# Softmax steps and key split of the second attention block re-ordered, and ScalarE's copy of the weighted values put ahead of a normalization in all later blocks

## The chip, the cores and the metric

The kernel runs on one core of a Trainium2 chip. The metric is device time in microseconds (us) of one execution. In the core, TensorE (PE) multiplies matrices into PSUM banks, VectorE (DVE) and ScalarE (ACT) take results out of PSUM and do elementwise work, GpSimd (POOL) does elementwise work on SBUF, and SyncE (SP) issues most DMA transfers. Each engine runs its instructions in the order of its queue.

## The reference

Four layers follow one another on 1024 tokens of 256 features (4 sequences of 256), each added to its input and normalized. The change touches only the first, attention with 16 heads:

```python
q = hidden_states @ Wq.T
k = hidden_states @ Wk.T
v = hidden_states @ Wv.T
# per head: 128 plain and 64 rotary features of q and k, 128 of v
q_rope = _apply_rope(q_rope, cos, sin)
k_rope = _apply_rope(k_rope, cos, sin)
scores = einsum('bqhd,bkhd->bhqk', q_nope, k_nope) / sqrt(DN) \
       + einsum('bqhd,bkhd->bhqk', q_rope, k_rope) / sqrt(DR)
attn = softmax(scores, axis=-1)
out = einsum('bhqk,bkhd->bqhd', attn, v)
return out.reshape(B, S, H * DV) @ Wo.T
```

After it come a gated feed-forward layer with a Walsh-Hadamard transform, an mLSTM block with its own feed-forward part, and a feed-forward layer with int8 weights. All results are float32.

## The kernel before

**Blocks.** Attention is cut into 16 blocks. Block h works on a pair of heads (h // 2) and one half of the tokens (h % 2: two sequences, 512 tokens). The main loop runs h = 0 to 14 and calls `first_block` for h = 0 and `fast_block` for the others; "the second block" is h = 1. A block computes the scores and softmax of its own pair and half, the projections of block h + 1, and the weighted values and output product of block h - 1, all interleaved. So the softmax of block h feeds the products V of block h + 1.

**Projections.** From h = 1 on they are the steps W0, W1 (values), R0, R1 (rotary parts of queries and keys), Q0, Q1 (plain queries of the two heads) and K0, K1 (plain keys). Each is two sums in two PSUM banks, built from inputs (`xp`) and weights (`wp`) that were split into a top part, a low part and a combination of them (`heads_of` L142, `rests_of` L156 to L158: three VectorE operations and a ScalarE cast per weight, then the DMA of the next pair's raw weight on SP). ScalarE copies the first bank (L521), VectorE joins the second to it (L523, L524). The bank is then free for the next step with the same tag. For rotary parts VectorE shuffles (L538), and GpSimd does three operations (L541 to L543).

**Softmax.** `scores` fills four banks, two with tag sc (first sequence, heads 0 and 1) and two with tag pt (second sequence): four quarters, numbered 0 to 3. `maxima` (VectorE, L610) takes the row maxima, `exponentials` (ScalarE, L619) the exponentials and their sums. `finish(k)` normalizes quarter k (reciprocal L627 on VectorE, multiplication on VectorE for even k, L632, on ScalarE for odd k, L630) and transposes it in blocks of 32 (VectorE, L640). `spread` then moves all four with 16 DMAs from SP into `prT`.

**Values and output.** `V00` to `V11` multiply prT with the values of the block before (first digit: sequence, second: head; L72 into `ps_ot`). After the second head ScalarE copies the sum to `oT` (`settled["across"]`, L687). `O0` and `O1` multiply oT with the output weight (L72 into `ps_mm`); each stands twice in the order, for its two halves of rows.

**What sets the order.** PE's order is written out by hand: `in_turn` ties each product behind the one before. In the second block it is `SECOND`, in the others `ORDER`:

```python
SECOND = "R0 W0 R1 W1 Q0 Q1 V00 V01 K0 V10 V11 K1 O0 O0 O1 O1".split()
ORDER = "W0 V00 V01 V10 V11 O0 O0 R0 R1 O1 O1 Q0 Q1 K0 K1 W1".split()
```

On the other engines a scheduler sets the order when the kernel is built, by the order of the code and its own estimate of when operands are ready, and `behind(ins)` puts what is traced under it behind `ins`, where both are on the same engine; it adds no wait of its own between engines. A block under `behind` that spans several engines is thus bound only on the engine of `ins`.

Of the kernel before, what the change touches and what calls it, by code (L numbers as in the profile page):

```python
# [23 lines left out]
NPAIR = H0 // 2  # L24
# [17 lines left out]
def tile_two_layers(ctx: ExitStack, tc: tile.TileContext, a: dict, out: bass.AP):  # L42
# [6 lines left out]
    def bank(tag):  # L49
        return psum.tile([P, 512], F32, tag=tag, name=f"ps_{tag}")  # L50
# [28 lines left out]
    def slot(k, shape, name, dtype=F32):  # L79
        return wts.tile(shape, dtype, tag=f"ff{k}", name=name)  # L80
# [6 lines left out]
    ps = bank("pt")  # L87
# [50 lines left out]
    def heads_of(p, name):  # L138

        top = attn.tile([P, KC, S], F32, tag="top", name="top")  # L140
        x, t = (raws[p, name], top) if name != "R" else (halves_first(raws[p, name]), pairs_first(top))
        return top, nc.vector.tensor_single_scalar(t.bitcast(I32), x.bitcast(I32), TOP, ALU.bitwise_and)  # L142
# [38 lines left out]
    def load_output(p):  # L181
        wo = attn.tile([P, 2, D], F32, tag="wo", name="w_o")
        nc.sync.dma_start(wo, a["w_o"][p])
        return wo
# [35 lines left out]
    settled = {}  # L220
    behind = lambda ins: tc.issue_after(ins.ins)
# [386 lines left out]
    def maxima(ps):  # L608
        nmax = small.tile([P, 2], F32, tag="nmax", name="nmax", bufs=5)
        nc.vector.tensor_reduce(  # L610
            nmax, ps.rearrange("p (t k) -> p t k", t=2), AX.X, ALU.max, negate=True
        )
        return nmax

    def exponentials(ps, nmax):
        pr = attn.tile([P, 2, S], F32, tag="pr", name="pr", bufs=5)
        rsum = small.tile([P, 2], F32, tag="rsum", name="rsum", bufs=5)
        for qt in range(2):
            nc.scalar.activation(  # L619
                pr[:, qt, :], ps[:, qt * S : (qt + 1) * S], AF.Exp,  # L620
                bias=nmax[:, qt : qt + 1], accum_out=rsum[:, qt : qt + 1],
            )
        return pr, rsum
# [18 lines left out]
    def spread(cross):  # L642

        prT = attn.tile([P, 2, 2, QB, 2, 2, 32], F32, tag="prT", name="prT")
        for c in range(QB):
            for r in range(QB):
                nc.sync.dma_start(
                    prT[32 * r : 32 * r + 32, :, :, c],
                    cross[32 * c : 32 * c + 32, :, r : XB : QB],
                )  # L650
        return {
            bb: [lambda kt, bb=bb, e=e: prT[:, bb, kt, :, e].rearrange("p c t q -> p t c q") for e in range(2)]
            for bb in range(2)
        }

    def crossing():
        return attn.tile([P, 2, XB, 2, 2, 32], F32, tag="cross", name="cross")
# [16 lines left out]
    def weighted(t, bb, e, probs, po):  # L674
        in_turn(
            lambda: mm_k(
                po[:, e * S : (e + 1) * S],
                lambda i: t[4][:, 2 * bb + i, e * P : (e + 1) * P],
                probs,
                2,  # L680
            )
        )

    def output_product(h, bb, po):

        oT = attn.tile([P, 2, S], F32, tag="oT", name="oT")
        settled["across"] = nc.scalar.copy(oT, po.rearrange("p (e s) -> p e s", e=2))  # L687
        p, n = divmod(h, 2)

        def halves():  # L690
            ps = bank("mm")
            for t in range(2):
                in_turn(
                    lambda: mm_k(
                        ps[:, t * D : (t + 1) * D],
                        lambda i: oT[:, i, t * P : (t + 1) * P],
                        lambda i: w_os[p][:, i, :],
                        2,
                    )
                )  # L700
                if not t:
                    yield
            rows = acc[n][:, 2 * bb : 2 * bb + 2, :]
            yield nc.vector.tensor_tensor(rows, ps.rearrange("p (t d) -> p t d", t=2), rows, ALU.add)

        steps = halves()
        return lambda: next(steps, None)
# [5 lines left out]
    def finisher(found, crossed):  # L713
        def finish(k):
            bb, e = divmod(k, 2)
            return block_transposed(normalized(*found[k], e), e, crossed[:, bb])
        return finish
# [31 lines left out]
    def fast_block(h, t, probs, prev, steps):  # L749

        po, outs, last = {}, {}, {}

        def take_step(name):
            last[name] = steps[name]()
            settled["block"] = last[name][1]
            return last[name]

        def value_step(bb, e):
            if not e:
                po[bb] = bank("ot")  # L760
            weighted(prev, bb, e, probs[bb][e], po[bb])
            if e:
                outs[bb] = output_product(h - 1, bb, po[bb])

        p = (h + 1) // 2
        ps = scores(t, (0, 1), (lambda: take_step("R0")) if h == 1 else nothing)
        crossed = crossing()
        top = [maxima(ps[bb][e]) for bb in range(2) for e in range(2)]
        found = [exponentials(ps[0][0], top[0])]
        finish = finisher(found, crossed)  # L770
        finish(0)
        for step in SECOND if h == 1 else ORDER:
            if step[0] == "V":
                value_step(int(step[1]), int(step[2]))
            elif step[0] == "O":
                settled["out"] = outs[int(step[1])]()
            elif step not in last:
                take_step(step)
            if step == "W0":
                copied, done = last["W0"]  # L780
                with behind(copied):
                    found.append(exponentials(ps[0][1], top[1]))
                    if h == 1:
                        found.append(exponentials(ps[1][0], top[2]))
                        found.append(exponentials(ps[1][1], top[3]))
                with behind(done):
                    finish(1)
            elif step == "R1" and h == 1:
                with behind(last["R1"][1]):
                    finish(2)  # L790
            elif step == "W1" and h == 1:
                with behind(last["W1"][1]):
                    settled["softmax"] = finish(3)
                out = spread(crossed)
            elif step == "V01" and h > 1:
                with behind(settled["across"]):
                    found.append(exponentials(ps[1][0], top[2]))
                finish(2)
            elif step == "V11" and h > 1:
                with behind(settled["across"]):  # L800
                    found.append(exponentials(ps[1][1], top[3]))
                settled["softmax"] = finish(3)
                if h > 1 and h % 2 and p < NPAIR:
                    with behind(settled["softmax"]):
                        split(p, "K")
                out = spread(crossed)
        return out

    def split(p, *names):
        tops = []  # L810
        for name in names:
            tops.append(heads_of(p, name))
        for name, (top, _) in zip(names, tops):
            last = rests_of(p, name, top)
        return last
# [25 lines left out]
    for h in range(NB - 1):  # L841
        if h:
            probs = fast_block(h, tiles, probs, prev, steps)
        else:
            probs = first_block(tiles, steps)
        with behind(settled["block"]):
            if h == 0:
                split(1, "Q", "K")
            elif h == 1:
                input_parts_of(1)  # L850
            elif h % 2 == 0 and h // 2 + 1 < NPAIR:
                split(h // 2 + 1, "R", "Q")
            if h % 2 and h // 2 + 2 < NPAIR:
                split(h // 2 + 2, "W")
        if h == 1:
            w2 = ff_weight("w2", 4)
            w2b = slot(3, [P, NH, D], "w2b")
        if h % 2 == 0:
            if 0 < h < NB - 2:
                w_os[h // 2 + 1] = load_output(h // 2 + 1)  # L860
        if h in (7, 9, 11):
            src, dst = (w2, w2b) if h == 7 else (dst, src)
            butterflies(1 << (h - 7) // 2, src, dst)
        prev, tiles = tiles, after_it
        if h + 2 < NB:
            after_it, steps = fast_projections(h + 2)
# [25 lines left out]
    ps, prs, outs = {}, {}, []  # L892
    for bb in range(2):
        ps.update(scores(tiles, (bb,)))
        top = [maxima(ps[bb][e]) for e in range(2)]
# [723 lines left out]
    split = tc.alloc_tile_pool(name="split", bufs=2, side="right")  # L1619
# [121 lines left out]
```

## Time and profile before

| what | value |
|---|---|
| median of three runs | 688.52 us |
| runs | 686.74, 688.93, 688.52 us |
| profiled execution | 689.46 us |
| its span, first to last instruction | 687.7 us |
| mean granted TensorE clock | 0.992 |
| busy share PE, DVE, ACT, POOL | 98%, 73%, 46%, 27% |
| score products of h = 1, 2, 3 start at | 37.88, 65.98, 89.81 us |

In the profile's rows a line number is that of the instruction in the kernel, or of a helper that many callers share (L72 is such a line). A timeline row gives start, duration, engine, line, operation, what is written and read, the count of merged instructions, and in brackets the idle time before it with what ended that. A row of the chain gives start, length and what filled that part of the chain. In a row of time slices the engines stand in the order PE, weight loads, DVE, ACT, POOL, then the granted TensorE clock, the DMA share and GB/s. A busy PE may still be slow or wait inside a merged row, so lengths of equal groups are compared.

### The profile page before, as it was taken

The numbers are of one execution on the slowest core, as the hardware profiler recorded it, in microseconds if no ns is written. First come the engines' busy times: TensorE is split into PE (matmuls) and PEld (weight loads), VectorE is DVE, ScalarE is ACT, GpSimd is POOL, SyncE is SP. The second block draws the span as 40 slices with busy tenths as digits, with TensorE's granted clock in tenths as the row PEclk, the third lists the DMA queues.
The fourth block names the chain that finished last, engine by engine and source line by source line (L and its number), as shares of the span: only waits on it lengthen the run. The fifth ranks groups of instructions, "written<-read, shape, count | busy, mean of one in ns | idle before, by whom it ended". The sixth has DMA issues, their size and how long they took to land.

```text
span 687.7 us, 9902 instructions
## 1 busy us (share of the span) xinstructions
PE 671.4 (98%) x3364; PEld 530.5 (77%) x3364; DVE 503.3 (73%) x1226; ACT 318.9 (46%) x823; POOL 187.4 (27%) x167
## 2 busy tenths in 40 slices
PE   9989999999999999999999999999999999999995
PEld 5878888888888888888888778745684568788785
DVE  6997777687787778777766796465679557966767
ACT  4545554554465455445535455156312651261652
POOL 4262224404426444364144410005000220000310
PEclk9999999999999999999999999999999999999998
DMA  7242334223332421431232540003121300001001
GB/s 247 90 93 52 111 85 92 49 68 84 66 85 51 108 62 40 99 78 31 47 62 51 195 101 34 1 0 124 40 84 62 123 1 1 0 1 62 0 1 62
DMA packets 56643, 45.44 MB, mean 66 GB/s; under 512 B 9968, under 2 KB 52112, under 8 KB 55440
## 3 DMA queue, kind: packets, MB, share of 16 engines
q1 hardware_dynamic: 55728, 41.00, 23.4%
q0 software_dynamic: 432, 3.15, 1.3%
q10 hardware_dynamic: 432, 0.66, 0.3%
q8 instruction: 27, 0.44, 0.3%
q14 instruction: 24, 0.20, 0.1%
HBM read 25.61 MB, written 1.08 MB: 39 GB/s over the span
## 4 chain that ended last, share of the span: by engine, by line
PE 81%; DVE 12%; ACT 4%; issue 1%; DMA 1%; POOL 0%; DVEq 0%; ACTq 0%
PE ps_mm L72 10%; PE ps_sc L515 8%; PE ps_d L72 7%; PE ps_ot L72 7%; PE ps_pt L515 5%; PE ps_d L1128 4%; PE ps_sc L587 4%; PE ps_pt L587 4%; PE ps_m L1069 4%; PE ps_d L1477 3%; PE ps_d L1069 3%; PE ps_mm L515 3%; PE ps_ot L556 3%; PE ps_mm L556 3%; PE ps_sc L599 2%; PE ps_m L72 2%
## 5 line engine op out<-in xcount | busy, mean ns | idle before, releaser
L541 POOL TENSOR_TENSOR rope_raw<-rope_raw,cst 128x512 f32<-128x512 f32 x28 | 38.4, 1370 | 203.8 <-DVE rope_swp L538 203.8
L515 PE MATMUL ps_sc<-xp,wp 128*128 128x512 f32 x246 | 69.3, 417 | 0.0
L72 PE MATMUL ps_mm<-w_o,oT 128*128 128x256 f32 x256 | 61.3, 384 | 1.7 <-ACT oT L687 1.4
L72 PEld LDWEIGHTS ps_mm<-w_o,oT 128*128 128x128 f32 x256 | 47.5, 189 | 13.2 <-ACT oT L687 6.9
L640 DVE STREAM_TRANSPOSE cross<-pr 128x512 f32<-128x512 f32 x60 | 42.3, 708 | 19.5 <-ACT pr L630 18.9
L72 PE MATMUL ps_ot<-prT,v 128*128 128x256 f32 x240 | 54.8, 380 | 0.5 <-issue 0.5
L515 PEld LDWEIGHTS ps_sc<-xp,wp 128*128 128x128 f32 x246 | 47.0, 192 | 9.5
L619 ACT ACTIVATE pr<-ps_sc,nmax 128x256 f32<-128x256 f32 x64 | 29.7, 472 | 50.0 <-DVE nmax L610 50.0
L1351 POOL TENSOR_TENSOR ex<-cst,ex 128x512 f32<-128x512 f32 x16 | 19.7, 1265 | 112.0 <-DMA ex<-far 112.0
L72 PEld LDWEIGHTS ps_ot<-prT,v 128*128 128x128 f32 x240 | 44.5, 190 | 6.8 <-issue 1.2
L515 PE MATMUL ps_pt<-xp,wp 128*128 128x512 f32 x162 | 41.5, 391 | 0.0
L542 POOL TENSOR_TENSOR rope_swp<-rope_swp,cst 128x512 f32<-128x512 f32 x28 | 36.4, 1299 | 0.0
L630 ACT ACTIVATE pr<-pr,rinv 128x256 f32<-128x256 f32 x60 | 27.2, 501 | 19.0 <-DVE rinv L627 18.9
L515 PEld LDWEIGHTS ps_pt<-xp,wp 128*128 128x128 f32 x162 | 30.4, 188 | 6.5
L610 DVE TENSOR_REDUCE nmax<-ps_sc 128x2 f32<-128x512 f32 x32 | 20.6, 686 | 15.6 <-PE ps_sc L599 15.5
L619 ACT ACTIVATE pr<-ps_pt,nmax 128x256 f32<-128x256 f32 x64 | 30.1, 485 | 2.8 <-DVE nmax L610 2.8
L587 PE MATMUL ps_sc<-kn,qn 128*128 128x256 f32 x128 | 30.3, 379 | 0.0
L587 PE MATMUL ps_pt<-kn,qn 128*128 128x256 f32 x128 | 30.2, 379 | 0.0
L72 PE MATMUL ps_d<-fm,w 128*128 128x512 f32 x64 | 29.4, 599 | 0.0
L1027 ACT ACTIVATE glu_g<-ps_d 128x512 f32<-128x512 f32 x16 | 9.5, 593 | 42.1 <-PE ps_d L72 42.1
L156 ACT CAST wp<-top 128x512 fp32r<-128x512 f32 x28 | 16.6, 618 | 26.7 <-DVE top L142 26.7
L1128 PE MATMUL ps_d<-w,hT 128*128 128x256 f32 x128 | 28.4, 379 | 0.0
(350 smaller groups left out, 1586.6 us busy)
## 6 DMA issues: line engine op xcount, KB each, us to landing
prT<-cross SPq DMA_DIRECT2D x240, 64.0 KB, 2.1
ex<-far SPq DMA_DIRECT2D x8, 512.0 KB, 5.4
w<-in_w SPq DMA_DIRECT2D x3, 1024.0 KB
w_o<-in_w_o SPq DMA_DIRECT2D x8, 256.0 KB, 5.1
rawR<-in_w_qkv SPq DMA_DIRECT2D x14, 128.0 KB, 2.6
rawW<-in_w_qkv SPq DMA_DIRECT2D x7, 256.0 KB, 3.0
rawQ<-in_w_qkv SPq DMA_DIRECT2D x7, 256.0 KB, 3.2
rawK<-in_w_qkv SPq DMA_DIRECT2D x7, 256.0 KB, 4.1
```

The lines of the kernel that those rows point to most:

```text
L72: last = nc.tensor.matmul(ps, lhsT=lhs(i), rhs=rhs(i), start=(i == 0), stop=(i == n - 1))
L515: lambda: nc.tensor.matmul(ps[at], lhsT=left(k, i), rhs=right(k, i), start=(m == 0), stop=(m == len(terms) - 1))
L541: nc.gpsimd.tensor_tensor(by_b(raw), by_b(raw), cs, ALU.mult)
L542: nc.gpsimd.tensor_tensor(by_b(swp), by_b(swp), sn, ALU.mult)
L556: lambda: nc.tensor.matmul(ps[at][:, t * S : (t + 1) * S], lhsT=xp[k][:, i, j * P : (j + 1) * P], rhs=part[:, k, i, :], start=(m == 0), st ...
L587: lambda: nc.tensor.matmul(ps[bb][e][:, qt * S : (qt + 1) * S], lhsT=qn[:, e, queries(bb, qt)], rhs=kn[:, e, keys(bb)], start=(qt == 0), s ...
L619: nc.scalar.activation(pr[:, qt, :], ps[:, qt * S : (qt + 1) * S], AF.Exp, bias=nmax[:, qt : qt + 1], accum_out=rsum[:, qt : qt + 1],)
L630: nc.scalar.mul(pr[:, qt, :], pr[:, qt, :], rinv[:, qt : qt + 1])
L640: return nc.vector.transpose(cross[:, :, e], pr.rearrange("p t (x i) -> p x t i", i=32))
L1069: nc.tensor.matmul(banks[name][:, batch(x)], lhsT=left, rhs=right, start=start and not x, stop=True, skip_group_check=True,)
L1128: lambda: nc.tensor.matmul(po, lhsT=hT[:, i, j * P : (j + 1) * P], rhs=wd[:, i, :], start=(i == 0), stop=(i == NH - 1),)
L1477: nc.tensor.matmul(ps, lhsT=lhs, rhs=rhs, start=(k == 0), stop=(k == len(terms) - 1))
```

## The change

In the second block the first quarter's normalization is no longer emitted right after its exponentials but behind W0's join. Exponentials 1, 2 and 3 go behind the copies of W0, R1 and W1 (before: all behind W0's). The finishes of quarters 0 to 3 go behind the joins of W0, R1, Q0 and Q1 (before: free, W0, R1, W1), and `spread` is emitted after Q1 and not after W1. The split of the second pair's key weights moves from the end of the first block (behind its last VectorE addition) into the second block, behind W1's join.

In the blocks from h = 2 the finish of quarter 1 is emitted at V01 and not at W0, and its ScalarE part is put behind the copy of the weighted values into oT; its VectorE part stays behind W0's join.

```diff
         found = [exponentials(ps[0][0], top[0])]
         finish = finisher(found, crossed)
-        finish(0)
+
+        def exponentials_behind(k, ins):
+            with behind(ins):
+                found.append(exponentials(ps[k // 2][k % 2], top[k]))
+
+        def finish_behind(k, ins):
+            with behind(ins):
+                settled["softmax"] = finish(k)
+
+        if h > 1:
+            finish(0)
         for step in SECOND if h == 1 else ORDER:
...
-            if step == "W0":
-                copied, done = last["W0"]
-                with behind(copied):
-                    found.append(exponentials(ps[0][1], top[1]))
-                    if h == 1:
-                        found.append(exponentials(ps[1][0], top[2]))
-                        found.append(exponentials(ps[1][1], top[3]))
-                with behind(done):
-                    finish(1)
-            elif step == "R1" and h == 1:
-                with behind(last["R1"][1]):
-                    finish(2)
-            elif step == "W1" and h == 1:
-                with behind(last["W1"][1]):
-                    settled["softmax"] = finish(3)
-                out = spread(crossed)
-            elif step == "V01" and h > 1:
+            if h == 1:
+                if step in ("W0", "R1", "W1"):
+                    copied, done = last[step]
+                    k = ("W0", "R1", "W1").index(step)
+                    exponentials_behind(k + 1, copied)
+                    if step == "W1":
+                        with behind(done):
+                            split(1, "K")
+                    else:
+                        finish_behind(k, done)
+                elif step in ("Q0", "Q1"):
+                    finish_behind(2 + int(step[1]), last[step][1])
+                    if step == "Q1":
+                        out = spread(crossed)
+            elif step == "W0":
+                exponentials_behind(1, last["W0"][0])
+            elif step == "V01":
                 with behind(settled["across"]):
-                    found.append(exponentials(ps[1][0], top[2]))
+                    finish_behind(1, last["W0"][1])
+                    exponentials_behind(2, settled["across"])
                 finish(2)
-            elif step == "V11" and h > 1:
-                with behind(settled["across"]):
-                    found.append(exponentials(ps[1][1], top[3]))
+            elif step == "V11":
+                exponentials_behind(3, settled["across"])
                 settled["softmax"] = finish(3)
...
             if h == 0:
-                split(1, "Q", "K")
+                split(1, "Q")
```

More of the change, by code (lines that the diff above doesn't have):

```diff
@@ L778, in fast_block @@
                 take_step(step)
-            if step == "W0":
-                copied, done = last["W0"]
-                with behind(copied):
-                    found.append(exponentials(ps[0][1], top[1]))
-                    if h == 1:
-                        found.append(exponentials(ps[1][0], top[2]))
-                        found.append(exponentials(ps[1][1], top[3]))
-                with behind(done):
-                    finish(1)
-            elif step == "R1" and h == 1:
-                with behind(last["R1"][1]):
-                    finish(2)
-            elif step == "W1" and h == 1:
-                with behind(last["W1"][1]):
-                    settled["softmax"] = finish(3)
-                out = spread(crossed)
-            elif step == "V01" and h > 1:
+            if h == 1:
[15 more added lines that the diff above has]
+            elif step == "V01":
                 with behind(settled["across"]):
-                    found.append(exponentials(ps[1][0], top[2]))
+                    finish_behind(1, last["W0"][1])
+                    exponentials_behind(2, settled["across"])
                 finish(2)
-            elif step == "V11" and h > 1:
-                with behind(settled["across"]):
-                    found.append(exponentials(ps[1][1], top[3]))
+            elif step == "V11":
+                exponentials_behind(3, settled["across"])
                 settled["softmax"] = finish(3)
-                if h > 1 and h % 2 and p < NPAIR:
+                if h % 2 and p < NPAIR:
                     with behind(settled["softmax"]):
```

## The prediction

> **What bounds the kernel now.** The page first: engine shares, then the chain that ended last.
>
> ```profile
> PE 671.4 (98%) x3364; PEld 530.5 (77%) x3364; DVE 503.3 (73%) x1226; ACT 318.9 (46%) x823; POOL 187.4 (27%) x167
> ...
> PE 81%; DVE 12%; ACT 4%; issue 1%; DMA 1%; POOL 0%; DVEq 0%; ACTq 0%
> ```
>
> PE is the bound, and the end moves only where PE stands still. So I followed the chain in order of time (start, length, what) through the second block (h = 1, scores from 37.9, next block's scores at 65.98) and an ordinary one (from 89.81):
>
> ```profile
> 38.84 2.74 DVE top L142 x2
> 41.58 2.31 DVE wp L157 x2
> ...
> 46.47 2.37 DVE nmax L610 x4
> ...
> 50.58 0.61 DVE v L523
> ...
> 51.23 0.97 PE ps_mm L556 x4
> 52.21 2.56 PE ps_sc L515 x6
> ...
> 100.30 1.99 PE ps_mm L72 x8
> ...
> 105.04 1.73 PE ps_mm L72 x8
> ```
>
> In the second block the chain leaves PE for DVE: splits of Q and K, row maxima, normalization, then the values' join (L523) that frees the bank W1 waits for. The six Q0 matmuls after it take 2.56 against 1.36 to 1.39 elsewhere. The last two lines are O0 and O1: same work, O0 0.26 longer. The waits of PE (us in total, times, longest):
>
> ```profile
> PE ps_mm L72 <- ACT oT L687: 1.4, 3, 0.5
> PE ps_mm L556 <- DVE v L523: 1.4, 1, 1.4
> PE ps_mm L556 <- ACT v L521: 0.8, 1, 0.8
> ```
>
> And the slices around the second block's stall (the figure after POOL is the granted clock):
>
> ```profile
> 50.00:51.00 1.00, 0.00 (x0) 0.00 (x0) 1.00 (x2) 1.00 (x5) 0.43 (x1) 1.00 0.00 0
> ...
> 52.00:53.00 1.00, 1.00 (x4) 0.81 (x4) 0.18 (x1) 1.00 (x3) 0.00 (x0) 0.50 0.00 0
> ```
>
> The stall cost twice: 0.8 + 1.4 of standing, then the clock: 0.78, 0.50, 0.50, 0.52 in the four us from 51, that is 0.22 + 0.50 + 0.50 + 0.48 = 1.7. Together 3.9.
>
> **Ordinary blocks (13, h = 2 to 14).** Why O0 is late, in the timeline:
>
> ```profile
> 98.72 0.12 DVE L627 RECIPROCAL rinv<-rsum 128x2 f32<-128x2 f32 x1
> 98.87 0.91 ACT L630 ACTIVATE pr<-pr,rinv 128x256 f32<-128x256 f32 x2 [0.98 <-DVE rinv L627]
> 99.69 0.56 ACT L687 COPY oT<-ps_ot 128x512 f32<-128x512 f32 x1
> ...
> 100.30 1.59 PEld L72 LDWEIGHTS ps_mm<-w_o,oT 128*128 128x128 f32 x8 [0.43 <-ACT oT L687]
> ```
>
> ScalarE stands 0.98 for the reciprocal, normalizes, and only then copies oT, though its product (V00, V01) left PE at 96.82 + 1.73 = 98.55. O0 reads that copy at 100.30. With the copy first it runs about 98.7 to 99.25, some 0.7 before V11 ends at 100.28: O0 follows without a gap, as O1 does. Gain: 13 x 0.26 = 3.4, plus the 1.4 of the three blocks where PE stood openly (h = 8, 10, 12): 4.8.
>
> What the moved wait holds up: ScalarE now stands at the copy until V01 ends; behind it are the normalization, two exponentials, the second copy. The copy leaves about 0.4 later than the reciprocal allows the normalization today, so the normalization ends near 100.0 instead of 99.73 and VectorE's transpose (99.81) starts 0.3 later; behind that transpose stands the reciprocal of the third quarter, which waits for an exponential until 101.21 anyhow. That exponential starts when copy and normalization are both done, now as before. Cover: 0.7 here; without it each us of lateness would be one at the prT transfers, which have (104.53 + 16 x 0.65 + 2.1 = 117.0, read by V00 at 120.66) 3.6 to spare. So nothing is charged. No DMA moves in these blocks.
>
> **The second block.** Removed from before the maxima: K's split. Its share of the two chain rows is half of 2.74 + 2.31, plus 0.6 of L158, about 3.1 at most; but Q's operations inherit some of the waiting on POOL that K's had. These lines show it:
>
> ```profile
> 20.81 0.41 DVE L142 TENSOR_SCALAR top<-rawR 128x512 int32<-128x512 int32 x1
> ...
> 40.08 1.50 DVE L142 TENSOR_SCALAR top<-rawK 128x512 int32<-128x512 int32 x1
> ...
> 57.53 1.29 DVE L640 STREAM_TRANSPOSE cross<-pr 128x512 f32<-128x512 f32 x2
> ```
>
> The same split step takes 0.41 alone and 1.50 while POOL turns the rotary keys; the two transposes took 0.64 each beside POOL too. So Q's L158 will wait as K's L142 did, maxima start at 44.6 instead of 46.37 (1.8 earlier), the values' copy at 46.2, W1's first bank is free before R1 ends at 47.8; the first normalization moves behind the values' join, which so ends near 47.7, before W1 asks for it at 48.9. Both stalls and the half clock go: up to 3.9.
>
> What is late next? First, K's split now runs between W1's join (about 51.7) and K0 (about 53.9), with three VectorE operations: 0.4 + 0.6 + 0.6 alone, 1.3 to 1.5 each beside POOL, whose key rotation (three of 1.29 to 1.33) falls just there. Ready at 53.3 to 55.7: K0 waits 0 to 1.4. Its DMA (rawK of the next pair, 0.6 on SP) moves with it, ahead of the probabilities' transfers. Second, and later: those transfers.
>
> ```profile
> 58.84 10.35 SPq L647 DMA_DIRECT2D prT<-cross  x16
> ```
>
> All 16 wait for the fourth transpose, take 10.35 to issue and 2.1 to land: 71.3, for V00 of the next block at 73.00. Slack 1.7, no more. The change puts the third and fourth quarters behind Q0's and Q1's joins and K's split ahead of them on VectorE. Counting VectorE's work from 38.76: Q's split 4.5 (to 43.3, just after POOL's last operation before it, 42.73); R0's join, shuffle and four maxima 3.7; W0's join and first quarter 2.0 to 2.9 (its two multiplications took 0.62 alone and 1.64 beside POOL); R1's join, shuffle and the second quarter's two operations 2.0; W1's join 0.6; K 1.5 to 4.0; Q0's and Q1's joins with two quarters 3.7 to 4.3, by how much of ScalarE's 0.9 of normalization shows. Sum 18.0 to 22.0: the fourth transpose ends between 56.8 and 60.8. I take the middle, 58.8, which is where it ends now (58.82): much the same work in a queue that is nearly full both ways. V00 then starts at 58.8 + 10.4 + 2.1 = 71.3 against 73.0: of the 3.9, 1.7 arrive. PE itself would be there at 69.1 plus K0's wait, so it stands 0.8 to 2.2, 1.5 in the middle. Bounds of the gain: 3.9 (transpose by 56.7) and -0.2 (60.8).
>
> **Two rules against rows.** The Trainium skill, SBUF — State Buffer, section "SBUF: two separate sides", says that VectorE and GpSimd share a port pair as an exclusive lock, the loser standing for the whole instruction. It speaks against this change, and 1.50 against 0.41 agrees; by it K's three would all wait, which is the upper end. The skill's TensorE: Matmul & The Clock Gate, section "Why this matters for your kernels", asks only for no idle gaps above about 3 us; the trace has half clock after gaps of 0.8 and 1.4. By the page no new wait here costs clock.
>
> By the rows it may: 2.2 of standing within 3.4 us brought a half-clock stretch that lost 1.7; the 0.9 lost before ps_ot at 380.7 brought none. 1.5 lies between; I charge none and keep 1.7 as a rival.
>
> **Sum.** 4.8 + 1.7 = 6.5 off the profiled execution: 689.46 (span 687.7) becomes 683.0. The median of the runs, 688.52, stands 0.94 under that execution, so 682.0. They spread from 686.74 to 688.93; a measurement can tell about 0.3%, 2.1 us.
>
> **Rivals.**
> Forecast, 682.0: 0.50.
> The second block gives all of its 3.9, because VectorE ends the fourth transpose by 56.7: 688.5 - 8.7 = 679.8. For it: POOL may be done before K's split. Against: the queue counted above. 0.17.
> The new wait at V00 (or at K0) is itself followed by half clock: 1.7 more, so 683.7. For it: the clock at 0.50 after 52. Against: the wait is shorter than that one. 0.18.
> O0's 0.26 doesn't go, because ScalarE's order comes out as it was or the delay is a restart of PE's weight load and not the copy: only the 1.7, 686.8, within 0.3%. Against: O1, whose copy is long done, shows none. 0.07.
> Slower: K's split and the two quarters behind it come so late on VectorE that prT lands long after V00 asks. Place: V00 of the third block; price: every us of the fourth transpose after 60.6 is one us, and 1.7 for the clock; it outweighs the 4.8 and the 2.1 of the bound once the transpose ends after 60.6 + 4.8 + 2.1 - 1.7 = 65.8. At 66.5: 688.5 - 4.8 + 5.9 + 1.7 = 691.3. For it: 1.7 of slack is all there is. Against: my latest sum is 60.8. 0.08.
> Faster thus 0.85, same 0.07, slower 0.08. The range 679.0 to 686.0 takes in the first three with some of the runs' spread and leaves out the last two.
>
> **What would show it.** Right: O0 and O1 both 1.73 in each ordinary block, block period 23.58 instead of 23.84, the oT copy ahead of the L630 pair on ScalarE; no wait of W1 on L521 or L523; clock 1.00 from 51 to 55; the first prT issue near 59 and PE waiting for prT at V00 of the third block. Wrong: O0 still at 1.99; the second block's successor starting its scores after 65; a half-clock window there; the fourth transpose before 56.8 (too careful) or after 60.8.

## The result, and the profile after

The changed kernel is slower: median 708.07 us (four runs, 705.39 to 710.44) against 687.63 us for the kernel before (four runs), a ratio of 1.0298 with a 95% interval of 1.0271 to 1.0325. The forecast was 682.0. The profiled execution took 707.18 with a span of 705.4, 17.7 more than the span before.

The page's first part, and the waits of PE (us in total, times, longest):

```profile
PE 677.4 (96%) x3364; PEld 536.8 (76%) x3364; DVE 510.7 (72%) x1226; ACT 319.2 (45%) x823; POOL 188.4 (27%) x167
```

```profile
PE ps_mm L515 <- DVE acc L704: 12.1, 6, 2.0
PE ps_ot L72 <- ACT pr L619: 2.1, 1, 2.1
PE ps_sc L515 <- DVE qn L524: 1.3, 1, 1.3
PE ps_ot L72 <- DMA prT<-cross: 0.9, 1, 0.9
```

The waits for oT (L687) and for the values in the second block (L521, L523) are gone from this list, as forecast. A new one stands at the top: six times PE waits 2.0 in the middle of Q1 (L515) for VectorE's addition L704. Six is the number of odd blocks from h = 3 to 13, those with a key split. Time slices from one block's scores to the next show it (time, PE, weight loads, DVE, ACT, POOL, then granted clock):

```profile
64.07:88.75 24.68, 23.80 (x125) 20.18 (x124) 17.55 (x36) 12.13 (x32) 7.62 (x6) 1.00 0.44 109
88.75:114.65 25.90, 23.88 (x126) 20.03 (x125) 20.76 (x39) 12.96 (x34) 8.54 (x6) 1.00 0.36 85
114.65:138.22 23.57, 23.57 (x127) 20.11 (x126) 16.33 (x33) 11.83 (x32) 7.63 (x6) 1.00 0.27 57
138.22:165.69 27.47, 25.45 (x126) 21.21 (x125) 20.75 (x39) 12.95 (x34) 8.52 (x6) 0.94 0.37 84
```

From h = 4 on the even blocks take 23.57, which is the forecast's 23.58. The odd ones take 25.90 once (h = 3) and 27.46 to 27.49 five times, the five with a mean clock of about 0.94. The difference adds up, from scores' start to scores' start:

| part | before | after | difference |
|---|---|---|---|
| to the third block's scores | 65.82 | 64.07 | -1.75 |
| seven even blocks, h = 2 to 14 | 168.33 | 166.10 | -2.2 |
| six odd blocks, h = 3 to 13 | 143.07 | 163.28 | +20.2 |
| from the last scores to the end | 310.47 | 311.98 | +1.5 |
| span | 687.7 | 705.4 | +17.7 |

How an odd block loses it stands in the chain that ended last (start, length, what), here in h = 3:

```profile
102.12 0.60 ACT rope_raw L521
102.72 0.74 ACT pr L630 x2
...
104.12 0.69 DVE cross L640
104.81 1.03 DVE top L142
105.84 0.60 DVE rope_raw L523
106.44 1.05 DVE wp L157
...
108.11 1.13 DVE wp L158
109.24 0.61 DVE acc L704
...
109.89 0.72 PE ps_mm L515 x2
```

Read it from below. The last two products of Q1 need the bank that O1 used, and O1's addition into acc (L704) frees it. On VectorE that addition stands behind the key split (L142, L157, L158); the split stands behind the fourth quarter's transpose (L640), because `split(p, "K")` is written behind `settled["softmax"]`; the transpose waits for the fourth quarter's normalization (L630), and that now stands behind R0's copy (L521). Before, the normalization was first (ScalarE, h = 3):

```profile
102.85 0.91 ACT L630 ACTIVATE pr<-pr,rinv 128x256 f32<-128x256 f32 x2 [0.28 <-DVE rinv L627]
103.67 0.58 ACT L521 ACTIVATE rope_raw<-ps_sc 128x512 f32<-128x512 f32 x1
```

The copy of oT, where the edit was made, is not in this chain at all. The order of a queue is fixed when the kernel is built, so this exchange is in the program; why the scheduler's estimate turned over is not visible in a trace.

On VectorE the same stretch, with the durations, and the first of GpSimd's operations beside it:

```profile
104.74 1.11 DVE L142 TENSOR_SCALAR top<-rawK 128x512 int32<-128x512 int32 x1
...
106.36 1.19 DVE L157 TENSOR_TENSOR wp<-rawK,top 128x512 fp32r<-128x512 f32 x1
...
108.11 1.13 DVE L158 SCALAR_TENSOR_TENSOR wp<-top,wp 128x512 fp32r<-128x512 f32 x1
109.16 0.68 DVE L704 TENSOR_TENSOR acc<-ps_mm,acc 128x512 f32<-128x512 f32 x1
...
104.30 1.27 POOL L541 TENSOR_TENSOR rope_raw<-rope_raw,cst 128x512 f32<-128x512 f32 x1 [15.79 <-DVE rope_swp L538]
```

And before, in the same block:

```profile
104.43 0.38 DVE L142 TENSOR_SCALAR top<-rawK 128x512 int32<-128x512 int32 x1
...
105.33 0.68 DVE L157 TENSOR_TENSOR wp<-rawK,top 128x512 fp32r<-128x512 f32 x1
...
106.56 0.67 DVE L158 SCALAR_TENSOR_TENSOR wp<-top,wp 128x512 fp32r<-128x512 f32 x1
...
107.74 0.68 DVE L704 TENSOR_TENSOR acc<-ps_mm,acc 128x512 f32<-128x512 f32 x1
...
106.74 1.64 POOL L541 TENSOR_TENSOR rope_raw<-rope_raw,cst 128x512 f32<-128x512 f32 x1 [16.87 <-DVE rope_swp L538]
```

Before, R0's shuffle came after the transpose, and GpSimd's turn (its rotation of R0's result) began at 106.74, when the split's last operation was already running. Now the shuffle is ahead of the transpose, GpSimd turns from 104.30 on, and the split runs beside it. With 3.43 instead of 1.73 for the three operations the addition comes too late for Q1.

### The profile page after: what moved, and what is told of

It reads as the page before. It is cut to its first block, busy times and chain, and to the rows that moved or that the text cites. A ratio compares the mean times of both kernels' runs of the same rounds, so it can differ in the third digit from the quotient of the medians.

```text
span 705.4 us, 9905 instructions
## 1 busy us (share of the span) xinstructions
PE 677.4 (96%) x3364; PEld 536.8 (76%) x3364; DVE 510.7 (72%) x1226; ACT 319.2 (45%) x823; POOL 188.4 (27%) x167
## 4 chain that ended last, share of the span: by engine, by line
PE 77%; DVE 14%; ACT 4%; issue 2%; POOL 1%; DMA 1%; DVEq 0%; ACTq 0%
PE ps_ot L72 8%; PE ps_mm L72 8%; PE ps_sc L515 7%; PE ps_d L72 6%; PE ps_pt L515 4%; PE ps_d L1138 4%; PE ps_sc L587 4%; PE ps_pt L587 4%; PE ps_m L1079 4%; PE ps_mm L556 3%; PE ps_d L1487 3%; PE ps_d L1079 3%; PE ps_ot L556 3%; PE ps_sc L599 2%; PE ps_m L72 2%; PE ps_mm L515 2%
## 5 line engine op out<-in xcount | busy, mean ns | idle before, releaser
L515 PE MATMUL ps_sc<-xp,wp 128*128 128x512 f32 x246 | 74.6, 441 | 1.3 <-DVE qn L524 1.3
L515 PEld LDWEIGHTS ps_sc<-xp,wp 128*128 128x128 f32 x246 | 49.9, 204 | 12.8 <-DVE qn L524 1.8
L72 PE MATMUL ps_ot<-prT,v 128*128 128x256 f32 x240 | 56.4, 388 | 3.0 <-ACT pr L619 2.1
L640 DVE STREAM_TRANSPOSE cross<-pr 128x512 f32<-128x512 f32 x60 | 42.2, 704 | 17.2 <-ACT pr L630 16.7
L515 PE MATMUL ps_pt<-xp,wp 128*128 128x512 f32 x162 | 43.0, 401 | 0.0
L515 PEld LDWEIGHTS ps_pt<-xp,wp 128*128 128x128 f32 x162 | 32.2, 199 | 7.5
L515 PE MATMUL ps_mm<-xp,wp 128*128 128x512 f32 x84 | 24.2, 411 | 12.2 <-DVE acc L704 12.1
L515 PEld LDWEIGHTS ps_mm<-xp,wp 128*128 128x128 f32 x84 | 15.4, 191 | 17.9 <-DVE acc L704 14.7
```

The costliest lines, as they stand in the source:

```text
L72: last = nc.tensor.matmul(ps, lhsT=lhs(i), rhs=rhs(i), start=(i == 0), stop=(i == n - 1))
L515: lambda: nc.tensor.matmul(ps[at], lhsT=left(k, i), rhs=right(k, i), start=(m == 0), stop=(m == len(terms) - 1))
L640: return nc.vector.transpose(cross[:, :, e], pr.rearrange("p t (x i) -> p x t i", i=32))
```

## The experiments

Theory A: the copy put first turns the order of R0 and the fourth quarter over, the key split meets GpSimd's turn, and the late addition holds Q1 up. Each run is beside runs of the kernel before (686.65 for the first four, 687.28 for the others).

**Only the ordinary blocks' part.** The second block is as before:

```diff
-                with behind(done):
-                    finish(1)
+                if h == 1:
+                    with behind(done):
+                        finish(1)
...
             elif step == "V01" and h > 1:
                 with behind(settled["across"]):
+                    with behind(last["W0"][1]):
+                        finish(1)
                     found.append(exponentials(ps[1][0], top[2]))
```

> Only the part for the blocks from h = 2: ScalarE's copy to oT ahead of the second quarter's normalization; the second block as before. Theory A (the order of the fourth quarter): the copy first lets the scheduler put R0's copy and join ahead of the fourth quarter's normalization and transpose, K's split in the odd blocks slides into POOL's turn, and O1's addition frees Q1's bank 2.2 late: odd blocks from h = 5 near 27.5 us, even ones 23.57, in all near 708. Rival B (the harm comes from the second block, its half-clock windows and the late prT going on through the blocks): this kernel is then faster than before, near 683.

Measured: 704.64 (699.18 to 708.64), ratio 1.025 (1.0207 to 1.0294). The loss is here, and rival B falls. Q1 waits as before, but the clock follows only in some blocks:

```profile
187.50:213.40 25.90, 23.88 (x126) 20.04 (x126) 20.74 (x39) 12.98 (x34) 10.24 (x9) 1.00 0.35 82
236.90:264.40 27.50, 25.48 (x127) 21.25 (x126) 20.75 (x39) 13.00 (x34) 11.79 (x11) 0.94 0.38 86
```

h = 3, 5 and 7 took 25.9 at full clock, h = 9, 11 and 13 27.5. "Near 27.5 from h = 5" was thus too high for two of the blocks. The second block, untouched here, shows something too. PE has the same two waits there as before (0.8 and 1.4), but the clock stays at 1.00, where the trace before has 0.50:

```profile
52.00:53.00 1.00, 1.00 (x6) 0.70 (x4) 0.28 (x1) 1.00 (x3) 0.00 (x0) 1.00 0.00 0
```

PE then waits 0.45 for W1's copy instead, and the block takes 27.16 and not 27.94.

**Only the second block's part.** From h = 2 on the order is as before:

```diff
             elif step == "W0":
                 exponentials_behind(1, last["W0"][0])
+                finish_behind(1, last["W0"][1])
             elif step == "V01":
-                with behind(settled["across"]):
-                    finish_behind(1, last["W0"][1])
-                    exponentials_behind(2, settled["across"])
+                exponentials_behind(2, settled["across"])
```

> Only the second block's part; from h = 2 on as before. Theory A: scores to scores of the second block 26.1 instead of 27.9, one wait of about 1 for prT in the third, every later block 23.84 or 24.3 as before, in all 0.5 to 1.0 below before, near 687. Rival B: most of the loss of 20 is here, near 705.

Measured: 687.98 (686.25 to 688.93), ratio 1.0008 (0.9996 to 1.002): no difference that can be told, where 0.5 to 1.0 below was expected. Scores to scores of the second block took 26.10, the third block 24.70, the later ones 23.83 to 24.30. Against the profiled execution before (27.94 and 23.83) that is 1.0 less in sum. Against the second block of the run above, which has the same two waits at full clock (27.16), it is nothing. The second block alone neither helps nor harms by more than can be told.

**The whole change, with R0 held behind the fourth quarter** (`settled["scaled"]` is the last ScalarE multiplication of a normalization):

```diff
+            elif step == "R0" and h > 1:
+                with behind(settled["scaled"]), behind(settled["softmax"]):
+                    take_step(step)
             elif step not in last:
                 take_step(step)
```

> The whole change, with R0's copy held behind the fourth quarter's normalization on ScalarE and R0's join behind its transpose on VectorE, which is the order of before. Theory A: odd and even blocks all 23.57, no wait of Q1, no half clock there, the wait at the first V after the loop back to 0.9: about 682. Rival C (the copy first is itself what is late, because ScalarE stands at it and everything behind slides): odd blocks stay above 26 and the time above 700.

Measured: 684.64 (683.74 to 685.02), ratio 0.9962 (0.9948 to 0.9977). Even blocks from h = 4 on took 23.57, odd ones 23.88 to 23.92, with no half clock. Putting back the order alone, with the copy still first, takes away the loss of 20. Rival C falls. The time is 2.6 above the expected 682. The odd blocks keep 0.3: the weight loads of Q1's last products still wait for O1's addition, six times, 0.5 at most. And the wait after the loop did not come back to what it was (the same row shows 0.5 before):

```profile
PE ps_ot L72 <- issue: 1.1, 1, 1.1
```

In h = 14 the fourth transpose starts 14.45 after the block's scores, 14.14 before, and the block itself is 0.27 shorter: together the 0.6 between the two rows.

**The whole change, with the key split early in the odd blocks.** R0 stays ahead of the fourth quarter:

```diff
-            finish(0)
+            first = finish(0)
...
             elif step == "W0":
                 exponentials_behind(1, last["W0"][0])
+                if h % 2 and p < NPAIR:
+                    with behind(first):
+                        split(p, "K")
...
-                if h % 2 and p < NPAIR:
-                    with behind(settled["softmax"]):
-                        split(p, "K")
```

> The whole change, with K's split in the odd blocks put behind the first quarter's transpose, where POOL rests, and not behind the fourth's. R0 still stands ahead of the fourth quarter. Theory A: O1's addition is early again, all blocks 23.57, but the fourth transpose stays 1.2 late, so the wait after the loop (2.5 and a half-clock window) remains: about 685.5. Rival D (the late fourth quarter itself holds PE up in the odd blocks, through prT or the exponentials' banks): odd blocks stay near 27.5.

Measured: 684.81 (682.93 to 685.35), ratio 0.9961 (0.9945 to 0.9978). All blocks from h = 3 to 14 took 23.57. The late fourth quarter does no harm by itself in a block; it harms through the split behind it. It does cost after the loop, as expected, where the trace shows the wait unchanged:

```profile
PE ps_ot L72 <- ACT pr L619: 2.0, 1, 2.0
```

The last block's prT is read by the first V after the loop sooner than elsewhere. Before, PE already stood there for 0.5, so every bit of lateness of the fourth transpose counts; here it starts 15.37 after the scores of h = 14 instead of 14.14. (The row names ScalarE's exponentials, which PE does not need there; the two-queue run below shows that it was the transfers.)

**Is it the port or the order?** VectorE's order is exactly that of the changed kernel in the odd blocks, but GpSimd doesn't turn these projections:

```diff
+            if n == 0 and h >= 4:
+                nc.scalar.copy((qr, kr)[c], swp)
+                rotated[h] = nc.gpsimd.tensor_copy((qr, kr)[c][:, 0:1], swp[:, 0:1])
+                return got
             by_b = lambda t: t.rearrange("p (b s) -> p b s", s=S)
```

> The whole change with VectorE's order untouched, but in the odd blocks from h = 3 GpSimd does not turn the rotary parts: ScalarE copies the shuffled half into place instead, and GpSimd writes one column (the rotation of these projections is left out). K's split then meets no GpSimd operation. Theory A1 (the port is the price): its three operations take 0.4, 0.7, 0.7 instead of 1.1, 1.2, 1.1, O1's addition comes 1.7 earlier, Q1's wait falls from 2.2 to about 0.5 and the half-clock windows in the odd blocks go: 707 - 6 x 1.7 - 5 x 1.7, about 688; the wait after the loop stays. Rival A2 (the order alone is the price: three operations more ahead of the addition, whatever they last): Q1 still waits about 2 and the time stays above 700.

Measured: 690.33 (689.25 to 691.19), ratio 1.0039 (1.0022 to 1.0055). The split in h = 3, and the wait:

```profile
104.11 0.38 DVE L142 TENSOR_SCALAR top<-rawK 128x512 int32<-128x512 int32 x1
...
105.01 0.68 DVE L157 TENSOR_TENSOR wp<-rawK,top 128x512 fp32r<-128x512 f32 x1
...
106.24 0.67 DVE L158 SCALAR_TENSOR_TENSOR wp<-top,wp 128x512 fp32r<-128x512 f32 x1
106.83 0.68 DVE L708 TENSOR_TENSOR acc<-ps_mm,acc 128x512 f32<-128x512 f32 x1
```

```profile
PE ps_mm L515 <- DVE acc L708: 2.2, 6, 0.4
```

The wait fell from 2.0 to 0.4 and the half clock in the odd blocks went. The odd blocks took 24.19 to 24.24, where at full clock they took 25.90 with the turn and 23.57 without a wait. So of the 2.3 lost, 1.7 is GpSimd's neighbourhood and about 0.65 the order itself. Theory A1 holds as far as GpSimd's work beside the split is the price; the run does not show what the two engines share. 2 us of the time stand above the expected 688, of which 1.4 lie behind the loop (313.45 from the last scores to the end, 312.00 in the run before this).

**The kernel before with that one exchange.** The copy to oT stays behind the normalization; the fourth quarter's normalization goes behind R0's copy, and the key split and the transfers, which are written behind it, move along in the code:

```diff
             elif step == "V11" and h > 1:
                 with behind(settled["across"]):
                     found.append(exponentials(ps[1][1], top[3]))
-                settled["softmax"] = finish(3)
+            elif step == "R0" and h > 1:
+                with behind(last["R0"][0]):
+                    settled["softmax"] = finish(3)
```

> The kernel before with one swap: from h = 2 on the fourth quarter's normalization stands behind R0's copy on ScalarE; the copy to oT stays behind the second quarter's normalization, the second block as before. Theory A: the swap alone makes K's split meet GpSimd: odd blocks 2.2 longer than 23.85, in some of them a half-clock window of 1.7 more, and the wait after the loop 1.5 longer: 701 to 711. Rival C (it takes the copy ahead of the normalization): blocks stay at 23.85 and the time near 687.

Measured: 708.7 (708.53 to 708.86), ratio 1.0308 (1.0287 to 1.033). Even blocks keep their 23.84, the odd ones take 26.19 or 27.73 to 27.79. On VectorE R0's join and shuffle stand ahead of the fourth transpose and GpSimd turns beside the split, as in the changed kernel; in h = 3 the split's operations take 1.13, 1.18 and 1.13. The exchange alone, without the copy to oT moved, makes the whole loss.

**Two versions with what was learned.** First: the early split, and four of the 16 prT transfers issued from ScalarE's queue in h = 1 and h = 14.

```diff
-                nc.sync.dma_start(
+                engine = nc.scalar if h in (1, NB - 2) and c == QB - 1 else nc.sync
+                engine.dma_start(
```

> Key split early in the odd blocks as in the run with 684.81, and in h = 1 and h = 14 four of the 16 prT transfers are issued from ScalarE's queue instead of SP's. If the 16 issues of 0.65 in one queue are what V00 waits for after the second block and after the loop, they end 2.6 earlier: the wait of 1.1 in the third block and the 2.35 after the loop with its half-clock window go: 684.8 - 1.1 - 2.35 - 1.7, about 679.7. If not the queue but the landing or the fourth transpose sets it, the time stays at 684 to 685.

Measured: 682.6 (682.26 to 683.96), ratio 0.9932 (0.9913 to 0.9951). The wait after the loop is gone, though the fourth transpose of h = 14 is as late as in the run with the early split (15.37 after the scores), which shows the queue of issues as its cause. The wait for prT in the third block is gone too; here that shows less, because PE itself comes there 0.4 later (V00 at 72.51 instead of 72.12). But 2.9 of the expected 679.7 are missing, 1.2 of it here:

```profile
PE ps_mm L72 <- ACT oT L688: 1.2, 1, 1.2
```

In the second block ScalarE's queue now stands at the transfers until the fourth transpose is done, and the second copy to oT stands behind them. In h = 14, too, ScalarE's copies stand behind the transfers, and the block takes 23.96 instead of 23.57. The rest of the 2.9 was not traced.

Second: in addition K0 is put behind V10 and V11 in the second block.

```diff
-    SECOND = "R0 W0 R1 W1 Q0 Q1 V00 V01 K0 V10 V11 K1 O0 O0 O1 O1".split()
+    SECOND = "R0 W0 R1 W1 Q0 Q1 V00 V01 V10 V11 K0 K1 O0 O0 O1 O1".split()
```

> As the run with two queues, and in the second block K0 stands behind V10 and V11 on PE. K0's wait of 1.3 for Q0's join and the 0.4 before it go, if PE's order is what made it: about 678. If prT of the third block is then the later one again, it gives less, 679 to 680.

Measured: 681.24 (680.53 to 682.36), ratio 0.991 (0.9894 to 0.9927), the fastest of all. K0's wait is gone, and V00 of the third block starts at 70.64 without a wait, earlier than 16 issues in one queue allowed (72.12): there, too, the queue was the cause. But the next block's scores now wait 0.9 for the keys' join (L523), whose copy stands behind the same transfers on ScalarE. The expected 678 was reckoned from 679.7, before the first version's 682.6 was known; 1.7 off that is 680.9, and the gain came close to it.

## Why the prediction was wrong

**The step that failed** is the last paragraph on the ordinary blocks, from "What the moved wait holds up" to "So nothing is charged". It followed the queues as they stood before the change: the delay of 0.3 on the second quarter ended at the third quarter's reciprocal. That much came true: in h = 14 the transposes of the four quarters start 8.43, 10.16, 12.40 and 14.14 after the block's scores before, and 8.43, 10.35, 12.12 and 15.36 now, so the second is 0.2 late, the third not, and the fourth 1.2. The order itself was taken as kept. It wasn't: with the copy first, R0's copy came ahead of the fourth quarter's normalization on ScalarE, and R0's join and shuffle ahead of its transpose on VectorE. Three sentences were then missing: that the key split stands behind that transpose in the odd blocks, that O1's addition stands behind the split, and that Q1 waits for the addition's bank. In the trace before, that addition ended at 108.35, and Q1's last two products, which need its bank, came some 0.5 later: 0.5 of cover, against the 3.6 for prT that were counted. The price was 2.3 in each of six blocks (25.90 against 23.57) and, in five of them, about 1.6 of half clock. (The 3.6 is too high as well: in h = 3 the transfer of a raw weight stands between the 16 issues, and the last one ends at 115.67, not at 104.53 + 16 x 0.65 = 114.9. That did not decide.)

**O0's gain was right.** 0.26 per block was forecast, 23.84 became 23.57 in the even blocks, and 24.31 to 24.33 became 23.57 in h = 8, 10 and 12.

**The second block was right in its mechanism and too high in its sum.** Both waits of W1 and the half clock went; scores of the next block start 1.75 earlier. VectorE's maxima started at 44.88 (44.6 forecast). K0 waited 1.3, within the 0 to 1.4, but for Q0's join (L524, ending at 56.9), which stood on VectorE behind the key split, and not for the split itself (ended at 56.3). The transfers then set the time:

```profile
60.03 10.35 SPq L647 DMA_DIRECT2D prT<-cross  x16
```

V00 of the third block started at 72.12 instead of 73.00. The term that was mis-sized is the fourth transpose: taken to end at 58.8, it ended at 59.99 (inside the stated 56.8 to 60.8), so 0.9 arrived and not 1.7. The wait of 0.9 there brought no half clock. In whole executions even that can't be told from nothing (1.0008). One reason is the 1.7 for the clock in the sum of 3.9: it was read from one execution. In two other traces with the second block as before, those of the runs with 704.64 and 708.7, the waits of 0.8 and 1.4 brought no half clock, and the block took 27.16 and 27.19. Against these the changed block's 26.12 gains only 1.1, and the third block gives as much back (24.68, and 23.57 in the first of these runs, which has the moved copy too).

**After the loop** prT had no spare time before either, which "3.6 to spare" overlooked; with the late fourth transpose the wait there grew from 0.5 to 2.1, and a half-clock stretch followed (the first product took 3.56 instead of 1.97). The table's last part grew by 1.5 only, because the profiled execution before has a half-clock stretch of its own near 563 us, about 1.7 lost, which the one after does not have.

**The rivals.** None of the five cases, the forecast among them, was what happened. The slower one had the direction right, but not the place: it put the key split and the late transpose into the second block, once, and not into six others. "ScalarE's order comes out as it was" asked the right question about the wrong instruction.

**The two rules.** That VectorE and GpSimd shut each other out, which the Trainium skill states (SBUF — State Buffer, "SBUF: two separate sides"), was weighed where the split was moved by hand and not where the scheduler moved it; the runs with and without the turn (1.11, 1.19, 1.13 against 0.38, 0.68, 0.67) agree with it. Of the advice on gaps above about 3 us (TensorE: Matmul & The Clock Gate, "Why this matters for your kernels") the measurement decides otherwise: waits of 2.0 were followed by half clock in five of six blocks of two traces and in three of six of a third. The same page states in its Part 1 that the activity window runs freely, 3413 ns long; a wait of 2.0 that is followed by half clock only sometimes agrees with that, though no run here moved the window on purpose.

## What to carry to other kernels

Where a scheduler sets the queues, an edit that moves one instruction is priced only when the new order of every queue around it is known: look at what now stands ahead of the longest work that is tied to a moved step, and pin the order where it matters. For each wait that PE does not show today, note how much cover it has; here the one with 0.5 of cover decided and not the one with 3.6. Long VectorE work on SBUF belongs into GpSimd's pauses: here the split's three operations took 3.43 beside GpSimd and 1.73 alone, while in the same rows of h = 3 joins that read PSUM (0.67 to 0.69) and transposes (0.69 to 0.71) took the same either way. Moving the split into such a pause undid the loss as well as putting the order back did (684.81 and 684.64); whether it would gain anything in the kernel before was not tried. And a half-clock stretch seen in one execution is not a term of every execution.

## What the runs showed of the hardware that was not expected

A single wait of 2.0 us on PE, as part of about 2.3 lost, can be followed by a half-clock stretch: the slices of one block give a mean clock of 0.94 over 27.5 us, about 1.6 us lost. It did not follow in h = 3, nor in h = 3, 5 and 7 of another run, with the same wait. So one program has blocks of 25.90 and 27.47 with equal work. Whole executions differ likewise: the four of the run with only the ordinary blocks' part took 699.18, 702.10, 707.18 and 708.64 us, with a mean granted clock of 0.996, 0.989, 0.984 and 0.980. Six stretches of 1.57 (27.47 less 25.90) would make 9.4, about the whole of that spread; how many each execution had is known only for the profiled one, 702.10, which had three.

In the first version with two queues, four transfers on ScalarE's queue took 2.88 us to issue (from 364.40 in h = 14), and its copies waited behind them; the other 12 took 7.97 on SP at the same time. Splitting issues over two queues is not free for the engine whose queue is used.
